# Segment attention with batch norm: four or six row tiles for each segment, chosen at run time

## The chip, the cores and the metric

The kernel runs on one core of a Trainium2 chip. A core has five engines that run their own instruction streams and wait for each other through semaphores: TensorE (matmuls, PE in the profile, its weight loads PEld), VectorE (DVE), ScalarE (ACT), GpSimd (POOL) and SyncE (SP, here only a queue for DMAs). The metric is device time in microseconds (us) of one execution. Three runs of the kernel before took 475.67, 477.01 and 477.55 us; the median, 477.01, is what the change is compared with.

## What is computed

There are 16384 tokens of 256 features, each with a segment id from 0 to 7. Ids are not sorted. A binary search over the ids gives each segment a start, and a token's slot is its index less that start; a token whose slot falls outside 0 to 3071 (negative ones wrap round) has none, and of several tokens on one slot one wins. Attention runs inside each segment over the slots that a token owns, with 32-wide queries and keys; then come a matmul with Wt, normalization over all tokens, relu, and the residual.

```python
q = feat @ Wq; k = feat @ Wk; v = feat @ Wv
starts = searchsorted(bids, arange(8))
pos = arange(N) - starts[bids]
qp, kp, vp = (zeros((8, 3072, c)).at[bids, pos].set(x) for x in (q, k, v))
scores = where(mask[:, None, :], einsum('bld,bmd->blm', qp, kp), -1e9)
rp = einsum('blm,bmd->bld', softmax(scores), vp)
t = rp[bids, pos] @ Wt
tn = (t - t.mean(0)) / sqrt(t.var(0) + 1e-5) * gamma + beta
out = feat + relu(tn)
```

On the reference's inputs the eight segments own 436, 511, 542, 726, 701, 698, 431 and 468 slots, 4513 in all. All other tokens read an empty slot, or one that another token owns.

## The kernel before

The function is segment_attention_bn_kernel. Rows of a segment are kept in FT = 6 row tiles of 128 (FW = 768 rows), whatever it owns; rows beyond the count are zero and are masked as keys. Four stages follow each other.

*Preparation* (lines 625 to 800, pool pp): loads of ids and weights, the binary search on VectorE, the counts n_bc of each segment and the running counts lcx. The longest segment becomes a register value (L794, L806), and L812 branches on it: the short path below, or a general path that these inputs don't take.

*Setting up the short path* (L813 to 846): the tiles xs (all tokens' rows, 48 row tiles), tk (results), acc (sums for the moments), xL, L, E and others are allocated and filled with zeros, xs by GpSimd (L831), the rest by VectorE (L832 to L837).

*Attention*, for segments 0 to 7 in one straight stream. load_list(e) (L859) builds a segment's list of tokens: masks ge and oh on VectorE (L866, L869), matmuls pc (L890), comparisons upto (L901), indices idx (L906), and then gathers by GpSimd of six row tiles of xs and of six columns reads_r (L911, L915, all through L850). project(b) (L917) transposes xs (px, L926), and makes queries and keys (pqk, L941), copied to q and k, and values (pv, L957; Wv and Wt have been multiplied together). attend(b) (L978) goes through two halves of 384 query rows: scores s (L994), four key tiles side by side on different rows of TensorE, then two; Exp by ScalarE into pr (L1000, two buffers); then for each of three query tiles six accumulating matmuls po (L1006), the reciprocal and the scaled row tk, and the two sums of acc (L1012 to L1023). After each half tk goes to DRAM (t_rows, L1038). reference_row (L964) subtracts a common row, from segment 0. The token tables (L1043 on) are worked out on VectorE after segment 0; load_others follows segment 1, and edge_selection (L1162) follows segment 2. The order within a block of straight code is made at build time by a scheduler, with program order as priority: ready work of later steps is drawn into gaps of earlier ones. Work inside a branch is not mixed with work outside it.

*The dense pass* (L1224 to 1359): every token's feature row is loaded, the relu of a common row is added and it is written back (f, L1299, L1320), while the rows of the lists are normalized (L1281 to L1287) and scattered into the output by GpSimd (L1336). A switch of many arms on GpSimd alone picks the order of the scatters.

The loop of attention, as it stands before the change:

```python
for b in range(NB):
    if b + 1 < NB:
        project(b + 1)
    if b + 2 < NB:
        load_list(b + 2, FT, xs[:, ts(b + 2, FT), :])
    attend(b)
```

Of the kernel before, what the change touches and what calls it, by code (L numbers as in the profile page):

```python
# [18 lines left out]
P = 128  # L19
# [12 lines left out]
QC = 384  # L32
QT = QC // P
# [497 lines left out]
def segment_attention_bn_kernel(  # L531
# [37 lines left out]
    LAST = TT * P - QC  # L569
# [5 lines left out]
    with ExitStack() as short:  # L575
# [13 lines left out]
        nc.vector.memset(eps_t, EPS)  # L589
        ones = keep.tile([P, P], F32, name="ones")  # L590
# [14 lines left out]
        arm_i = keep.tile([1, 1], I32, name="arm_i")  # L605
        ident = keep.tile([P, P], F32, name="ident")
        ecol = keep.tile([P, NB], F32, name="ecol")
        b_f = keep.tile([P, J], F32, name="b_f")

# [15 lines left out]
        with ExitStack() as prep:  # L625
# [46 lines left out]
            nc.vector.tensor_scalar(later_part[:, 1:2], part_i, 2 * NE, None, ALU.is_ge)  # L672

# [120 lines left out]
            nc.vector.tensor_copy(most_i, most)  # L794
            nc.vector.tensor_copy(cbeg, ps_c[:, 0, :])
# [16 lines left out]
        with tc.If(n_max < FW):  # L812
            with ExitStack() as path:  # L813
                fs = path.enter_context(tc.tile_pool(name="fs", bufs=1))
                xs = fs.tile([P, TT, D], F32, name="xs")
                tk = fs.tile([P, TT, D], F32, name="tk")
                idx = fs.tile([P, TT + LT], I32, name="idx")
                reads_r = fs.tile([P, TT], F32, name="reads_r")
                valid = fs.tile([P, TT + LT], F32, name="valid")
                mask = fs.tile([P, TT], F32, name="mask")  # L820
                rdens = fs.tile([P, TT], F32, name="rdens")
                acc = fs.tile([P, 2, D], F32, name="acc")
                sref = fs.tile([P, D], F32, name="sref")
                eidx = fs.tile([P, 1], I32, name="eidx")
                late = fs.tile([P, QT, P], F32, name="late")
                wE = fs.tile([NE, P], F32, name="wE")
                E = fs.tile([P, 2, D], F32, name="E")
                xL = fs.tile([P, LT, D], F32, name="xL")
                L = fs.tile([P, LT, D], F32, name="L")
                ridL = fs.tile([P, LT], I32, name="ridL")  # L830
                nc.gpsimd.memset(xs, 0.0)  # L831
                nc.vector.memset(acc, 0.0)  # L832
                nc.vector.memset(xL, 0.0)
                nc.vector.memset(ridL, NB * FW)
                nc.vector.memset(L, 0.0)
                nc.vector.memset(E, 0.0)
                nc.vector.memset(reads_r, 0.0)  # L837

# [8 lines left out]
                parts = {}  # L847
# [11 lines left out]
                def load_list(e, T, x):  # L859

# [3 lines left out]
                    ge = fw.tile([P, FW], F32, tag="ge", name=f"ge_{e}", bufs=1)  # L864
                    oh = fw.tile([P, FW], F32, tag="oh", name=f"oh_{e}", bufs=1)
                    nc.vector.tensor_scalar(  # L866
                        ge[:, 0 : T * P], ir, lcx[:, e, J : J + 1], None, ALU.is_ge
                    )
                    nc.vector.scalar_tensor_tensor(  # L869
                        oh[:, 0 : T * P], ir, cend[:, e : e + 1], ge[:, 0 : T * P],  # L870
# [6 lines left out]
                    if e < NB:  # L877
                        nc.vector.tensor_scalar(
                            mask[:, own_t], valid[:, own_t], 1.0, -NEG, ALU.subtract, ALU.mult
                        )  # L880
                    pad = fw.tile([P, FT], F32, tag="pad", name=f"pad_{e}")
                    nc.vector.tensor_scalar(
                        pad[:, 0:T], valid[:, own_t], 1.0, -float(N), ALU.subtract, ALU.mult
# [33 lines left out]
                def project(b):  # L917


                    x, v = xs[:, ts(b, FT), :], vs[b % 2]  # L920
                    xT = fw.tile([P, DH, FW], F32, tag="xT", name=f"xT_{b}", bufs=1)
                    for c in range(FT // 2):
                        for h in range(DH):
                            px = ps_a.tile([P, 2 * P], F32, tag="px", name=f"px_{b}")
                            for t in range(2):
                                nc.tensor.transpose(  # L926
                                    px[:, ts(t, P)], x[:, 2 * c + t, ts(h, P)], ident
                                )
                            if h == 0:
                                nc.scalar.copy(xT[:, h, ts(c, 2 * P)], px)  # L930
                            else:
                                nc.vector.tensor_copy(xT[:, h, ts(c, 2 * P)], px)


                    q = fw.tile([P, FW], F32, tag="q", name=f"q_{b}")
                    k = fw.tile([P, 2, P], F32, tag="k", name=f"k_{b}")
                    for c in range(FW // QC):
                        own_c = ts(c, QC)
                        pqk = ps_a.tile([P, QC], F32, tag="px", name=f"pqk_{b}")
                        for h in range(DH):  # L940
                            nc.tensor.matmul(  # L941
                                pqk, wqk[:, h, :], xT[:, h, own_c],
                                start=(h == 0), stop=(h == DH - 1),
                            )
                        nc.vector.tensor_copy(q[0 : 2 * DQ, own_c], pqk[0 : 2 * DQ, :])
                        nc.scalar.copy(q[2 * DQ : P, own_c], pqk[0 : 2 * DQ, :])
                        for u in range(QT):
                            t = c * QT + u
                            at, half = t % 4, P // 2 + DQ * (t % 2)
                            nc.vector.tensor_copy(  # L950
                                k[ts(at, DQ), t // 4, :], pqk[half : half + DQ, ts(u, P)]
                            )
                    for c in range(FT // 2):
                        pv = ps_a.tile([P, 2, D], F32, tag="px", name=f"pv_{b}")
                        for t in range(2):
                            for h in range(DH):
                                nc.tensor.matmul(  # L957
                                    pv[:, t, :], xT[:, h, ts(2 * c + t, P)], wvt[:, h, :],
                                    start=(h == 0), stop=(h == DH - 1),
                                )  # L960
                        nc.scalar.copy(v[:, 2 * c : 2 * c + 2, 0:D], pv)
                    parts[b] = (q, k)
# [15 lines left out]
                def attend(b):  # L978


                    q, k = parts[b]
                    v = vs[b % 2]
                    for c in range(FW // QC):
                        if b == NB - 1 and c == FW // QC - 1:
                            gather(E[:, 0, :], t_rows[0:LAST, :], eidx, LAST)
                            e_late = ps_a.tile([P, D], F32, tag="px", name="e_late")
                            root = fw.tile([P, 1], F32, tag="root", name="root")
                        pr = fw.tile([P, FT, QC], F32, tag="pr", name=f"pr_{b}")
                        for t0 in range(0, FT, 4):
                            quad = range(t0, min(t0 + 4, FT))  # L990
                            s = ps_s.tile([P, 4, PB], F32, tag="s", name=f"s_{b}")
                            for t in quad:
                                g = ts(t - t0, DQ)
                                nc.tensor.matmul(  # L994
                                    s[:, t - t0, 0:QC], k[g, t0 // 4, :], q[g, ts(c, QC)],
                                    start=True, stop=True,
                                )
                            for t in quad:
                                m = b * FT + t
                                nc.scalar.activation(  # L1000
                                    pr[:, t, :], s[:, t - t0, 0:QC], AF.Exp, bias=mask[:, m : m + 1]
                                )
                        for u in range(QT):
                            po = ps_o.tile([P, D + 1], F32, tag="po", name=f"po_{b}")
                            for t in range(FT):
                                nc.tensor.matmul(  # L1006
                                    po, pr[:, t, ts(u, P)], v[:, t, :],
                                    start=(t == 0), stop=(t == FT - 1),
                                )
                            at = b * FT + c * QT + u  # L1010
                            one = slice(at, at + 1)
                            nc.vector.reciprocal(rdens[:, one], po[:, D : D + 1])  # L1012
                            nc.vector.scalar_tensor_tensor(  # L1013
# [179 lines left out]
                for b in range(NB):  # L1193
                    if b + 1 < NB:
                        project(b + 1)
# [209 lines left out]
```

## Time and profile before

| What | Value |
|---|---|
| median of three runs | 477.01 us |
| span of the profiled execution | 474.8 us |
| PE busy | 361.2 us (76%) |
| DVE busy | 300.1 us (63%) |
| POOL busy | 174.6 us (37%) |
| ACT busy | 111.2 us (23%) |
| po matmuls (L1006), records | 576, 134.4 us |
| Exp (L1000) | 96, 577 ns each |
| gathers of xs and reads_r (L850) | 48 and 48, 1.05 us each |
| DMA moved | 53.14 MB |

The busy lines are shares of the whole span and average over stages with different limits, so the stages have to be read one by one. A line of the timeline gives the start, the duration, the engine, the source line, the operation with what it writes and reads, and in brackets how long its engine had been idle and whom it waited for. A float32 matmul shows as two records. A busy line of a stage gives each engine's busy time and, in parentheses, its instructions.

### The profile page before, as it was taken

The page shows a single profiled execution, that of the slowest core. Times are in us where ns is not written, and L with a number is a line of the kernel's source. Part 1 is how long each engine was busy: PE and PEld are TensorE (multiplying, and loading weights), DVE is VectorE, ACT ScalarE, POOL GpSimd, SP SyncE. Part 2 cuts the span into 40 slices and gives each one's busy share as a digit, 9 for nine tenths or more (in the row PEclk, how much of TensorE's full clock was granted, in tenths as well). Part 3 has the DMA queues.
Part 4 walks back from the last instruction along what each step waited for, and adds up shares of the span by engine and source line. Part 5 has one row for each costly group of instructions (what it writes and reads, how often), then busy time and mean ns, then how long its engine had stood idle before and what let it go on. Part 6 is the DMA issues. An engine that isn't in the chain of part 4 may idle for free. (4 is left out here: it accounts for less than half of the span.)

```text
span 474.8 us, 4852 instructions
## 1 busy us (share of the span) xinstructions
PE 361.2 (76%) x1465; PEld 237.1 (50%) x1465; DVE 300.1 (63%) x841; ACT 111.2 (23%) x232; POOL 174.6 (37%) x172
## 2 busy tenths in 40 slices
PE   4200368699999999999999999998891688989400
PEld 2000237467667667767677687676660243433200
DVE  6779868647879737446544644534447976977960
ACT  2000011223231432343243243324430011111000
POOL 1009360453804745407217127000002004667770
PEclk9999758979979999999999999999995566555555
DMA  5000100102312211203102101000119799999940
GB/s 92 1 6 0 34 10 1 44 4 65 101 50 68 68 48 51 77 0 94 35 0 72 34 27 49 33 2 33 55 56 381 318 351 421 378 416 412 413 170 8
DMA packets 21521, 53.14 MB, mean 112 GB/s; under 512 B 6670, under 2 KB 14176, under 8 KB 17386
## 3 DMA queue, kind: packets, MB, share of 16 engines
q1 hardware_dynamic: 10538, 24.98, 14.3%
q10 hardware_dynamic: 4224, 17.70, 9.8%
q0 software_dynamic: 6720, 10.03, 6.8%
q8 instruction: 14, 0.23, 0.2%
q14 instruction: 25, 0.20, 0.1%
HBM read 26.67 MB, written 29.92 MB: 119 GB/s over the span
## 5 line engine op out<-in xcount | busy, mean ns | idle before, releaser
L1006 PE MATMUL po<-vs,pr 128*128 128x257 f32 x576 | 134.4, 386 | 6.1 <-DVE acc L1023 5.0
L1006 PEld LDWEIGHTS po<-vs,pr 128*128 128x128 f32 x576 | 107.3, 191 | 32.7 <-ACT pr L1000 10.0
L850 POOL DMA_INDIRECT xs<-in_r_feat,idx x48 | 50.2, 1046 | 125.5 <-DVE upto L901 113.3
L1336 POOL DMA_INDIRECT out<-tk,idx x48 | 47.2, 984 | 52.6 <-DMA out<-f 34.2
L850 POOL DMA_INDIRECT reads_r<-reads_of,idx x48 | 51.0, 1062 | 14.6 <-issue 14.0
L1000 ACT ACTIVATE pr<-s,mask 128x384 f32<-128x384 f32 x96 | 48.7, 577 | 32.2 <-PE s L994 32.1
L1307 PE MATMUL pf<-y,hot 48*128 48x256 bf16 x128 | 35.2, 382 | 21.9 <-DVE f L1318 11.5
L1012 DVE RECIPROCAL rdens<-po 128x1 f32<-128x1 f32 x48 | 8.1, 168 | 64.2 <-PE po L1006 64.1
L957 PE MATMUL pv<-wvt,xT 128*128 128x256 f32 x192 | 46.5, 394 | 0.4
L994 PE MATMUL s<-q,k 32*128 32x384 f32 x192 | 44.3, 540 | 2.1 <-DVE k L950 2.1
L957 PEld LDWEIGHTS pv<-wvt,xT 128*128 128x128 f32 x192 | 36.7, 196 | 10.7 <-issue 5.9
L1318 DVE TENSOR_TENSOR f<-f,pf 128x512 f32<-128x512 f32 x48 | 30.9, 681 | 15.8 <-PE pf L1307 15.7
L1022 ACT ACTIVATE sq<-tk 128x256 f32<-128x256 f32 x48 | 20.0, 417 | 85.2 <-DVE tk L1013 72.5
L1307 PEld LDWEIGHTS <-hot 48*128 48x128 bf16 x128 | 13.7, 118 | 49.2 <-issue 45.8
L1312 PE MATMUL pf<-f,ident 128*128 128x256 f32 x64 | 36.0, 673 | 0.0
L926 PE MATMUL px<-ident,xs 128*128 128x128 f32 x96 | 19.7, 318 | 15.3 <-DMA xs<-in_r_feat,idx 7.5
L941 PE MATMUL pqk<-xT,wqk 128*128 128x384 f32 x64 | 28.0, 590 | 0.0
L890 PE MATMUL pc<-lcx,oh 128*128 128x130 f32 x102 | 16.3, 301 | 13.9 <-DVE oh L869 13.9
L926 PEld LDWEIGHTS px<-ident,xs 128*128 128x128 f32 x96 | 12.0, 154 | 28.4 <-issue 9.9
L1316 ACT COPY f<-pf 128x512 f32<-128x512 f32 x16 | 9.4, 585 | 71.2 <-PE pf L1312 71.2
L930 ACT COPY xT<-px 128x256 f32<-128x256 f32 x24 | 9.0, 373 | 69.2 <-PE px L926 69.2
L1013 DVE SCALAR_TENSOR_TENSOR tk<-po,rdens,sref 128x256 f32<-128x256 f32 x48 | 23.1, 481 | 1.5
(228 smaller groups left out, 406.9 us busy)
## 6 DMA issues: line engine op xcount, KB each, us to landing
f<-in_r_feat SPq DMA_DIRECT2D x16, 1024.0 KB, 9.8
out<-f ACTq DMA_DIRECT2D x16, 1024.0 KB, 9.1
t_rows<-tk SPq DMA_DIRECT2D x16, 384.0 KB, 2.6
eb<-edge_of SPq DMA_DIRECT2D x16, 96.0 KB, 2.9
xs<-in_r_feat,idx POOLq DMA_INDIRECT x48, 2.8
reads_r<-reads_of,idx POOLq DMA_INDIRECT x48, 2.4
out<-tk,idx POOLq DMA_INDIRECT x48, 8.4
wv_sb<-in_L_rec_Wv ACTq DMA_DIRECT2D x1, 256.0 KB, 3.2
```

The source lines that it names most:

```text
L850: nc.gpsimd.indirect_dma_start(out=dst, out_offset=None, in_=table, in_offset=bass.IndirectOffsetOnAxis(ap=ind, axis=0), bounds_check=n - ...
L926: nc.tensor.transpose(px[:, ts(t, P)], x[:, 2 * c + t, ts(h, P)], ident)
L941: nc.tensor.matmul(pqk, wqk[:, h, :], xT[:, h, own_c], start=(h == 0), stop=(h == DH - 1),)
L957: nc.tensor.matmul(pv[:, t, :], xT[:, h, ts(2 * c + t, P)], wvt[:, h, :], start=(h == 0), stop=(h == DH - 1),)
L994: nc.tensor.matmul(s[:, t - t0, 0:QC], k[g, t0 // 4, :], q[g, ts(c, QC)], start=True, stop=True,)
L1000: nc.scalar.activation(pr[:, t, :], s[:, t - t0, 0:QC], AF.Exp, bias=mask[:, m : m + 1])
L1006: nc.tensor.matmul(po, pr[:, t, ts(u, P)], v[:, t, :], start=(t == 0), stop=(t == FT - 1),)
L1013: nc.vector.scalar_tensor_tensor(tk[:, at, :], po[:, 0:D], rdens[:, one], sref, ALU.mult, ALU.subtract,)
L1307: nc.tensor.matmul(pf[:, u, :], hot[r, g % (NG // 2), i + u, :], y3[r, :], start=True, stop=not on_pe,)
L1312: nc.tensor.matmul(pf[:, u, :], ident, two[:, u, :], start=False, stop=True)
L1318: nc.vector.tensor_add(two, two, pf)
L1336: w = nc.gpsimd.indirect_dma_start(out=out, out_offset=bass.IndirectOffsetOnAxis(ap=idx[:, at : at + 1], axis=0), in_=y, in_offset=None, b ...
```

## The change

Every segment is given as many row tiles as it needs, out of two choices: four (TMIN) if it owns fewer than 512 slots, six otherwise. The choice is made at run time. For each half of the segments (PART = 4) a small number with one bit for each segment is counted (tiles_i), and attention becomes two switches of 16 arms, one for each combination; each arm holds the whole stream of four segments. It is for leaving out row tiles that hold nothing but zeros. Lists, gathers, and the projection of segments 0 and 4 keep six tiles in any case.

With it go these edits. Scores are taken 512 query rows wide (pr_a) and, for six tiles, 256 more (pr_b); both are single buffers. first_scores(b) takes the scores of the first four key tiles right after the projection, at the end of the segment before. Queries, keys and xT get fixed tiles; keys are copied ahead of queries. The zeros of xs, tk, acc, E, xL and L are written by ScalarE during preparation, before the branch, so the pool fs is opened earlier; tk needs zeros now in tiles that are not computed. The token tables split in two, the second part (edge_tables) after segment 1; load_others and edge_selection move to segments 2 and 4. The late matmuls of the last segment cover all its tiles instead of three, one behind each tile's sum. The rows of the other list are normalized in place (L instead of yL).

```diff
+            def zero(x):
+                nc.scalar.copy(x, nil.to_broadcast([P, x.shape[1]]))
+            for b in range(NB):
+                zero(xs[:, ts(b, FT), :].rearrange("p t d -> p (t d)"))
+            for b in range(NB):
+                zero(tk[:, b * FT + TMIN : (b + 1) * FT, :].rearrange("p t d -> p (t d)"))
+            for x in (acc, E, xL, L):
+                zero(x.rearrange("p t d -> p (t d)"))
...
+            nc.vector.scalar_tensor_tensor(
+                tiles, n_bc[0:1, 0:NB], float(TMIN * P), powers, ALU.is_ge, ALU.mult
+            )
+            nc.vector.tensor_reduce(
+                part, tiles.rearrange("x (a b) -> x a b", b=PART), AX.X, ALU.add
+            )
+            nc.vector.tensor_copy(tiles_i, part)
...
-                nc.gpsimd.memset(xs, 0.0)
-                nc.vector.memset(acc, 0.0)
-                nc.vector.memset(xL, 0.0)
-                nc.vector.memset(ridL, NB * FW)
-                nc.vector.memset(L, 0.0)
-                nc.vector.memset(E, 0.0)
-                nc.vector.memset(reads_r, 0.0)
...
+                pr_a = fw.tile([P, FT, QA], F32, name="pr_a", bufs=1)
+                pr_b = fw.tile([P, FT, FW - QA], F32, name="pr_b", bufs=1)
+                tiles = [
+                    nc.values_load(
+                        tiles_i[0:1, a : a + 1],
...
+                def scores(b, items):
+                    q, k = qs[b % 2], ks[b % 2]
+                    s = ps_s.tile([P, 4, PB], F32, tag="s", name=f"s_{b}")
+                    for i, (t, c, w) in enumerate(items):
+                        g = ts(t % 4, DQ)
+                        nc.tensor.matmul(
+                            s[:, i, 0:w], k[g, t // 4, :], q[g, c : c + w], start=True, stop=True
+                        )
...
+                def attend(b, T):
+                    w = (T - TMIN) * P
...
+                    if T > TMIN:
+                        scores(b, [(4, 0, QA), (5, 0, QA), (2, QA, w), (3, QA, w)])
+                        scores(b, [(0, QA, w), (1, QA, w), (4, QA, w), (5, QA, w)])
+                    for u in range(T):
+                        sums(b, u, T, e_late)
...
+                def project(b, T):
+                    turn(b, T)
+                    queries_keys(b, 0, QA)
+                    if T > TMIN:
+                        queries_keys(b, QA, (T - TMIN) * P)
+                    values(b, T)
...
                 load_list(0, FT, xs[:, ts(0, FT), :])
-                project(0)
+                project(0, FT)
+                first_scores(0)
                 reference_row()
                 load_list(1, FT, xs[:, ts(1, FT), :])
...
+                for a in range(NB // PART):
...
+                    for arm in tc.Switch(tiles[a], 1 << PART):
+
+                        T = [FT if arm >> i & 1 else TMIN for i in range(PART)] + [FT]
+                        for i in range(PART):
+                            b = a * PART + i
+                            if b + 1 < NB:
+                                project(b + 1, T[i + 1])
+                            if b + 2 < NB:
+                                load_list(b + 2, FT, xs[:, ts(b + 2, FT), :])
+                            attend(b, T[i])
+                            if b + 1 < NB:
+                                first_scores(b + 1)
+                            if b == 0:
+                                token_tables()
+                            if b == 1:
+                                edge_tables()
+                            if b == 2:
+                                load_others()
+                            if b == 4:
+                                edge_selection()
...
-                yL = fin.tile([P, LT, D], F32, name="yL")
...
-                    normal(yL[:, two, :], xL[:, two, :], L[:, two, :], min(2, LT - at))
+                    normal(L[:, two, :], xL[:, two, :], L[:, two, :], min(2, LT - at))
```

## The prediction

> **What bounds the kernel now.** I read the 40 slices first, then busy time by stage, then the order of instructions inside stages.
>
> ```profile
> PE   4200368699999999999999999998891688989400
> PEld 2000237467667667767677687676660243433200
> DVE  6779868647879737446544644534447976977960
> ```
>
> TensorE is full from slice 12 to 27, VectorE is fuller before that, and both are uneven in the last quarter. Columns below: stretch, its length, then busy us (instructions) of PE, PEld, DVE, ACT, POOL, then clock, DMA share, GB/s.
>
> ```profile
> 34.50:86.40 51.90, 25.13 (x88) 17.19 (x88) 42.28 (x111) 4.45 (x10) 23.02 (x15) 0.80 0.04 10
> 86.40:125.00 38.60, 34.13 (x148) 24.80 (x149) 22.59 (x88) 10.73 (x23) 21.45 (x21) 0.91 0.19 50
> 125.00:165.50 40.50, 39.14 (x165) 26.79 (x163) 33.52 (x89) 13.23 (x29) 19.37 (x17) 0.92 0.22 68
> 165.50:232.20 66.70, 65.94 (x304) 47.97 (x304) 33.96 (x110) 23.89 (x52) 30.44 (x30) 1.00 0.17 49
> 232.20:330.90 98.70, 96.91 (x441) 69.61 (x439) 45.95 (x141) 35.96 (x77) 23.93 (x24) 1.00 0.11 34
> 330.90:353.40 22.50, 20.70 (x101) 15.31 (x100) 10.31 (x27) 8.37 (x18) 1.00 (x1) 1.00 0.13 41
> 353.40:474.80 121.40, 70.75 (x201) 30.70 (x200) 85.61 (x154) 11.77 (x20) 53.43 (x54) 0.55 0.82 323
> ```
>
> These are: start up to the first sum of attention; segment 0; segment 1; 2 and 3; 4 to 6; 7; the dense pass. From 165.5 to 330.9 TensorE works 98% of the time: its work is the price. The dense pass moves data (DMA share 0.82). The order of the start:
>
> ```profile
> 34.34 0.14 DVE L794 CAST most_i<-most 1x1 int32<-1x1 f32 x1
> 35.54 10.34 POOL L831 MEMSET xs<- 128x12288 f32 x1 [32.91 <-issue]
> ...
> 38.17 8.12 DVE L866 TENSOR_SCALAR ge<-iota_r,lcx 128x768 f32<-128x768 f32 x1
> ...
> 47.41 0.61 DVE L866 TENSOR_SCALAR ge<-iota_r,lcx 128x768 f32<-128x768 f32 x1
> ...
> 53.86 1.20 POOL L850 DMA_INDIRECT xs<-in_r_feat,idx  x1 [7.51 <-DVE upto L901]
> ```
>
> The same operation lasts 8.12 us while GpSimd fills, 0.61 later. From 34.34 to the first gather at 53.86 nothing else can start. TensorE in a steady segment (33.4 us long):
>
> ```profile
> 213.34 8.10 PE L1006 MATMUL po<-vs,pr 128*128 128x257 f32 x36
> 221.37 0.93 PE L994 MATMUL s<-q,k 32*128 32x384 f32 x8
> ...
> 234.95 2.85 PE L941 MATMUL pqk<-xT,wqk 128*128 128x384 f32 x8
> ...
> 238.67 5.71 PE L957 MATMUL pv<-wvt,xT 128*128 128x256 f32 x24
> 244.22 1.78 PE L890 MATMUL pc<-lcx,oh 128*128 128x130 f32 x12
> ```
>
> Each float32 matmul is two records. By tile, 212.5 to 245.9 has po 16.45, s 5.48, pv 5.66, pqk 2.85, px 1.91, pc 1.74 us.
>
> **What the skill says.** "SBUF — State Buffer", section "SBUF: two separate sides": GpSimd and a VectorE operation in a two-port mode share a port pair under an exclusive lock, so the later one waits out the whole instruction. The trace agrees: 8.12 us against 0.61. "TensorE: Matmul & The Clock Gate", Part 3: matmuls on different 32-row groups run side by side. Agreed: four of s as one group take 0.93 us, two take 0.91. "Runtime: NRT & Kernel Launch", "Instruction fetch mechanics": a taken branch outside the fetched window waits until a DMA has brought the target. This trace shows no such branch by itself.
>
> **The change, part by part.** *How many tiles.* On the reference's inputs the segments own 436, 511, 542, 726, 701, 698, 431, 468 slots. Four (0, 1, 6, 7) are under 512 and take four tiles; 0 is still projected with six.
>
> *Sums of a short segment.* 16 products instead of 36: 16.45 x 16/36 = 7.3 us. pv: 5.66 x 4/6 = 3.8; pqk the same way 1.9; px 1.3; pc stays 1.74. Scores: one group of four, 512 wide: 0.92 x 512/384 = 1.2 us if side by side. Together 17.2, plus 1 us of gaps as now: 18.2 instead of 33.4. *A long segment*: three score groups, 1.2 + 1.2 + 0.6; together 31.7 and 1 of gaps: 32.7, nearly as now.
>
> *Start.* The GpSimd fill and six VectorE fills leave this place; ScalarE writes nearly all zeros before the branch, VectorE the two small ones. The price, from "ScalarE: Activation LUTs", section "What ACT_TABLE_LOAD costs" (186 ns and 0.833 ns an element): eight of 1536 elements 1.47 us, ten of 512 0.61, two of 768 0.83: 19.5 us, an estimate. ScalarE is busy 2.8 of the first 34.5 us, so it is hidden. ge then ends at about 37.3 instead of 46.2: 8.9 saved. The token tables (L1049 and on), now inside the arms, no longer cut in before upto (1.2) and between pqk and k (2.5), and Exp of segment 0, whose scores now go ahead of the reference row, no longer starts 1.7 before the first sum. Against it 0.5 for the counting operations (three of some 0.14 and a load). Net 13.8 saved, before the switch.
>
> *Two switches.* Each engine jumps by itself. From below, the branch at L812 took 1.07 us with its load (34.48 to 35.55 on VectorE); from above, add a fetch like a DMA's landing (eb 2.9 us) and a cold TensorE clock for some us: 6. I take 3.5 for the first, where segment 1's gather is waited for anyway, and 5 for the second. All later work of each engine queues behind its jump. First sum at 86.4 - 13.8 + 3.5 = 76.1.
>
> *What the arms keep in.* The token tables can't fill VectorE's idle time before the switch any more: 12 passes of about 1.2 us, a reduction of 1.87 and small ones, 17.5. For segment 0 VectorE has these, a list 4 (ge 0.61, oh 1.01, six upto of 0.35, small ones), a projection 2.7 (two xT of 0.42, q 0.7, four k of 0.29) and four row tiles of sums at 1.7 (rdens 0.17, three operations of 0.48, gaps): 31. For segment 1: a list 4, a six-tile projection 4.1, sums 6.9 and the edge tables 6: 21. That is 52 against 39 of TensorE (17.5 and 21.6), so VectorE bounds this stage: with 6 of waits 58 us (79.1 now), to 134. Segments 2 and 3: 66, to 200. Switch: 205.
>
> *Part two.* Segment 4: projection 10.4, scores 3, sums 16.45, list 1.74 and a gap: 32.6. Segment 5 with the short projection of 6: 10.4 - 3.5 = 6.9, in all 29.1. Segment 6 without list and with 7's projection: 16.4. Segment 7: sums 7.3, four late matmuls 2.2, and 3 for Exp, which writes the single pr_a only after segment 6's sums: 12.5. Sum 90.6 (121.2 now), to 296. The edge selection (eight of 0.91 + 1.12, 16 us of VectorE) lies in segment 4: VectorE 35 against 32.6, which segment 5 (18 against 29) takes up. Moved pools, six late tables, and L in place of yL: nothing, beside TensorE or the dense pass.
>
> *Dense pass.* Unchanged: 121.4, and 1 for the join. 418 us of span. The timed median lies 2.2 above the profile's span: **420**.
>
> **Rivals.** (1) *Cheap jumps, VectorE hidden*: jumps of 2 us, segments 0 and 1 in 50: 407. For it: DVE is idle within every steady segment (17.39 of 33.4 busy). Against: the tables come all at once. 17%. (2) *Jumps that cost all through*: every block of 256 instructions is waited for (the Runtime page's block size): part one has some 900 on TensorE, both parts seven blocks, 2.9 each: 20 more, 440. For it: arms are large and padded. Against: straight code within an arm is fetched ahead. 19%. (3) *Slower than before*: pr_a is not doubled, so each segment's Exp (six of 0.7, with latencies 6 us) lies bare: 48 for eight, with (2) 420 + 68 = 488. Against: the next projection (7 to 10 us of TensorE) lies between. 4%. The forecast keeps 60%.
>
> **How the numbers follow.** The likeliest is 420. The low end, 404, takes in (1) with shorter waits; the high end, 442, the switches' upper price twice (7 more), VectorE's waits doubled (6) and much of (2). Outside remain (3) and tails of (1) and (2). Faster 0.95, same 0.01, slower 0.04.
>
> **What would show it.** ge near 0.6 us at about 36.5; 416 records of sums instead of 576 (4 x 16 + 4 x 36, twice); first sum near 76; segments 0 and 1 with DVE above 85%; short segments in part two 16 to 18 us; a hole of 3 to 6 us on all engines near 200; the dense pass 121. It is wrong if the holes at the switches pass 10 us, if idle before po falls to pr (Exp) at every segment, or if the dense pass starts later than the sums' end allows.

## The result and the profile after

The changed kernel takes **437.26 us** (median of four runs, 434.82 to 438.22), the kernel before, measured beside it, 476.34: a ratio of 0.919, 95% interval 0.913 to 0.925. The forecast was 420, so the direction was right and 17 us of the expected 57 did not come. The profiled execution is the fastest of the four: 434.82 us, span 432.9. Some executions come out slower than the others of the same kernel, and the ratios, here and below, leave those out, so that a ratio can differ a little from that of the medians.

The slices of the page first, as for before:

```profile
PE   1143684996697999999599989999706888989200
DVE  6796124996962267556457954646479866596950
PEclk9996597998697799999579999999855675555555
```

A slice is now 10.8 us. TensorE is no longer full from one end of attention to the other: it dips to 5 in the twentieth slice (206 to 216 us). The granted clock is 0.6, 0.7 and 0.7 in three of the slices between 108 and 151 us, and 0.5 and 0.7 in the two from 206 on. The first of these slices lies in segments 0 and 1, the others are the places that the forecast lacks.

The stages, cut at the end of each segment's last sum (columns as in the prediction; the start up to the first sum, segments 0 and 1, 2, 3, the second switch with 4, 5, 6 and 7, dense pass):

```profile
33.80:75.70 41.90, 24.21 (x92) 15.92 (x93) 15.51 (x67) 6.30 (x13) 16.68 (x19) 0.74 0.09 23
75.70:127.20 51.50, 42.85 (x171) 29.98 (x169) 43.31 (x143) 11.07 (x24) 26.73 (x22) 0.88 0.11 34
127.20:169.70 42.50, 38.68 (x158) 26.52 (x158) 19.73 (x74) 12.64 (x27) 20.55 (x22) 0.88 0.21 63
169.70:203.60 33.90, 33.89 (x163) 24.88 (x162) 19.11 (x65) 12.26 (x26) 17.95 (x18) 1.00 0.18 53
203.60:249.50 45.90, 39.56 (x157) 26.24 (x157) 32.39 (x77) 14.57 (x28) 13.36 (x12) 0.85 0.21 64
249.50:280.00 30.50, 29.33 (x138) 21.16 (x138) 15.79 (x52) 10.98 (x24) 15.57 (x16) 1.00 0.14 43
280.00:307.30 27.30, 25.41 (x117) 18.11 (x116) 16.95 (x43) 10.77 (x22) 1.46 (x2) 1.00 0.13 44
307.30:432.90 125.60, 71.13 (x199) 30.30 (x198) 85.30 (x152) 11.17 (x18) 53.23 (x54) 0.54 0.81 315
```

Segments 2, 3 and 4 do nearly the same work on TensorE, six tiles each. Segment 3 takes 33.9 us with TensorE always busy at clock 1.00. Segment 2 takes 42.5 and segment 4 45.9, both at a lower clock, with idle time, and with more busy time for the same matmuls. The forecast against this table:

| Stage | Forecast, us | Measured, us | Difference |
|---|---|---|---|
| start to the first sum | 76.1 | 75.75 | -0.3 |
| segments 0 and 1 | 58 | 51.5 | -6.5 |
| segments 2 and 3 | 66 | 42.5 + 33.9 | +10.4 |
| second switch and segment 4 | 5 + 32.6 | 45.9 | +8.3 |
| segment 5 | 29.1 | 30.5 | +1.4 |
| segments 6 and 7 | 28.9 | 27.3 | -1.6 |
| dense pass and join | 122.4 | 125.6 | +3.2 |
| span | 418 | 432.9 | +14.9 |

The remaining 2.4 us lie between this execution (434.82, 1.9 above its span, where the forecast had 2.2) and the median of the runs.

The start of the changed kernel, in order of time, answers to the lines of before:

```profile
33.56 0.13 DVE L834 CAST most_i<-most 1x1 int32<-1x1 f32 x1
33.62 0.15 DVE L845 CAST tiles_i<-part 1x2 int32<-1x2 f32 x1
34.63 0.69 DVE L906 TENSOR_SCALAR oh<-iota_r,lcx 128x768 f32<-128x768 f32 x1 [0.87 <-DVE tiles_i L845]
...
40.20 1.20 POOL L892 DMA_INDIRECT xs<-in_r_feat,idx  x1 [5.29 <-DVE idx L952]
```

The comparison that took 8.12 us takes 0.69, and the first gather leaves at 40.20 instead of 53.86. The sums are 320 records on pr_a and 96 on pr_b, 416 as forecast.

TensorE around segment 2 (start, duration, what; in brackets its idle time and whom it waited for):

```profile
112.53 2.07 PE L1018 MATMUL s<-q,k 32*128 32x512 f32 x2 [4.84 <-DVE q L995]
...
135.97 0.90 PE L974 MATMUL px<-ident,xs 128*128 128x128 f32 x3 [2.69 <-DMA xs<-in_r_feat,idx]
...
141.00 5.37 PE L985 MATMUL pqk<-xT,wqk 128*128 128x512 f32 x8
```

and the same pqk one segment later:

```profile
177.91 2.75 PE L985 MATMUL pqk<-xT,wqk 128*128 128x512 f32 x8
```

A wait for the gathered rows of segment 3, then the same eight records at half speed. The gathers themselves, from GpSimd's timeline:

```profile
124.94 0.99 POOL L892 DMA_INDIRECT xs<-in_r_feat,idx  x1 [16.25 <-DVE upto L947]
126.24 1.18 POOL L892 DMA_INDIRECT xs<-in_r_feat,idx  x1 [0.30 <-issue]
127.73 1.19 POOL L892 DMA_INDIRECT xs<-in_r_feat,idx  x1 [0.30 <-issue]
129.22 1.00 POOL L892 DMA_INDIRECT reads_r<-reads_of,idx  x1 [0.30 <-issue]
...
133.12 1.00 POOL L892 DMA_INDIRECT xs<-in_r_feat,idx  x1 [0.30 <-issue]
```

GpSimd had been idle for 16 us until the list was ready (upto), so the gathers begin only as segment 2 begins; and three gathers of reads_r, which nobody waits for yet, stand ahead of the last three of xs.

At the second switch, ScalarE:

```profile
204.74 2.42 ACT L1023 ACTIVATE pr_a<-s,mask 128x512 f32<-128x512 f32 x4
211.41 1.28 ACT L1096 ACT_TABLE_LOAD   x1 [4.26 <-issue]
212.71 0.20 ACT L1096 ACTIVATE root<-eps_t 128x1 f32<-128x1 f32 x1
212.81 0.35 ACT L978 COPY xT<-px 128x256 f32<-128x256 f32 x1
...
217.39 1.28 ACT L1023 ACT_TABLE_LOAD   x1
...
316.08 1.28 ACT L1330 ACT_TABLE_LOAD   x1 [9.01 <-DVE mom L1328]
```

and TensorE there:

```profile
213.22 1.12 PE L974 MATMUL px<-ident,xs 128*128 128x128 f32 x4 [3.11 <-ACT xT L978]
...
218.52 4.09 PE L985 MATMUL pqk<-xT,wqk 128*128 128x512 f32 x8
```

"issue" means that the engine waited for nothing that the profile shows in the idle 4.26 us: this is the jump. VectorE shows 4.06 at the same place; TensorE stands for 2.61 us from 204.67 on. Behind the jump comes something that the forecast did not speak of. Before, the early square root that brings in its function table (L1036) read a column of sq, and so could only run at the end. Now it reads the constant eps_t (L1096) and depends on nothing, so the scheduler put it at the top of the arm: the table is loaded, the copy of xT waits behind it (TensorE waits 3.11 us for that copy), Exp has to load its table again, and at 316.08 the dense pass loads the square root's once more.

### The profile page after: what moved, and what is told of

It is laid out like the page before. It is cut to its first block, busy times and chain, and to the rows that moved or that the text cites. A ratio compares the mean times of both kernels' runs of the same rounds, so it can differ in the third digit from the quotient of the medians.

```text
span 432.9 us, 4300 instructions
## 1 busy us (share of the span) xinstructions
PE 313.1 (72%) x1195; PEld 197.4 (46%) x1195; DVE 274.3 (63%) x801; ACT 110.1 (25%) x205; POOL 167.8 (39%) x179
## 5 line engine op out<-in xcount | busy, mean ns | idle before, releaser
L1051 PE MATMUL po<-vs,pr_a 128*128 128x257 f32 x320 | 78.3, 391 | 2.9 <-ACT pr_a L1023 2.3
L1051 PEld LDWEIGHTS po<-vs,pr_a 128*128 128x128 f32 x320 | 59.3, 193 | 17.3 <-issue 4.4
L1018 PE MATMUL s<-q,k 32*128 32x512 f32 (+1 forms) x128 | 36.8, 593 | 6.0 <-DVE q L995 6.0
L1004 PE MATMUL pv<-wvt,xT 128*128 128x256 f32 x168 | 40.8, 398 | 0.0
L974 PEld LDWEIGHTS px<-ident,xs 128*128 128x128 f32 x84 | 11.7, 170 | 42.6 <-issue 19.6
L1023 ACT ACTIVATE pr_a<-s,mask 128x512 f32<-128x512 f32 x40 | 24.7, 687 | 17.8 <-PE s L1018 17.7
L978 DVE COPY xT<-px 128x256 f32<-128x256 f32 x21 | 8.9, 422 | 29.5 <-PE px L974 29.5
L985 PE MATMUL pqk<-xT,wqk 128*128 128x512 f32 (+1 forms) x52 | 25.4, 634 | 0.1
L1051 PE MATMUL po<-vs,pr_b 128*128 128x257 f32 x96 | 21.8, 381 | 0.3 <-DVE tk L1056 0.3
L992 DVE COPY k<-pqk 32x128 f32<-32x128 f32 x42 | 12.2, 291 | 14.0 <-PE pqk L985 13.1
L1390 PEld LDWEIGHTS pf<-f,ident 128*128 128x128 f32 x64 | 15.4, 292 | 12.2 <-issue 7.6
```

Source lines behind the costliest of these rows:

```text
L974: nc.tensor.transpose(px[:, ts(t, P)], xs[:, b * FT + t0 + t, ts(h, P)], ident)
L985: nc.tensor.matmul(pqk[:, 0:w], wqk[:, h, :], xT[:, h, own_c], start=(h == 0), stop=(h == DH - 1),)
L1004: nc.tensor.matmul(pv[:, t, :], xT[:, h, ts(t0 + t, P)], wvt[:, h, :], start=(h == 0), stop=(h == DH - 1),)
L1018: nc.tensor.matmul(s[:, i, 0:w], k[g, t // 4, :], q[g, c : c + w], start=True, stop=True)
L1023: nc.scalar.activation((pr_b if c else pr_a)[:, t, 0:w], s[:, i, 0:w], AF.Exp, bias=mask[:, m : m + 1],)
L1051: nc.tensor.matmul(po, pr[:, t, ts(r, P)], v[:, t, :], start=(t == 0), stop=(t == T - 1))
```

## The experiments

Each kernel is the changed one with the edit shown, but for the fourth. The first four ran on one chip, beside a kernel before of 474.63 us. The next four and the last four ran on two others, where the kernel before took 514.99 and 512.66 us; these two are alike, so ratios to the kernel before are set side by side, and stages of attention only where they differ by more than these groups do among themselves.

**Arms fixed when the kernel is built** (12 and 3, the arms that these inputs take): no switch is left, and work can be ordered across the borders.

```diff
-                    for arm in tc.Switch(tiles[a], 1 << PART):
+                    for arm in tc.Switch((12, 3)[a], 1 << PART):
```

> The two choices of an arm are made at build time (the arms that the inputs take, 12 and 3), so nothing is dispatched and the whole of attention is one block again. Theory A (jumps and block ends cost): the trace after has holes of 4.06 to 4.42 us on VectorE, ScalarE and TensorE at each jump, a cold clock behind the second, and the token tables can't be drawn forward; without them 437 falls to 420 to 427. Rival B (the single-buffered scores and VectorE's queue are the loss, the jumps are hidden beside waits for gathers): 433 to 437.

Measured: 422.88 us, ratio 0.882 (0.875 to 0.889); span 422.1. Theory A: by the medians 14.4 us, by the spans of the profiled executions 10.8, are the price of the two switches, with all that the scheduler orders otherwise when they are gone. The first sum comes at 72.4 instead of 75.75; segments 3 and 4 together take 72.6 us instead of 79.8. Part of the latter is not the jump: the square root on eps_t is drawn forward here too, but to 34.6 us, so that no table load stands in segment 4. Segment 2 is not better for it (44.0).

**The square root tied to data again**:

```diff
-                        nc.scalar.activation(root, eps_t, AF.Sqrt)
+                        nc.scalar.activation(root, E[:, 1, 0:1], AF.Sqrt)
```

> Only the input of the square root that loads ScalarE's table is changed, from a constant to the last result E, as the kernel before had it tied to the last sum. Theory A: the square root now runs first in the second arm, between the jump and the first xT copy, so one table load (1.28 us) stands there on the path of TensorE, and a third one stands ahead of root_v in the dense pass (1.28 us): 2.5 to 4 us less, 433 to 435. Rival B: both lie beside other waits (the pqk at a cold clock, the loads of f): 437, within 1.

Measured: 432.94 us, ratio 0.909 (0.903 to 0.915), 4.3 less than the changed kernel: theory A, a shade more than it named. ScalarE at the end of attention in this kernel:

```profile
306.24 0.42 ACT L1064 ACTIVATE sq<-tk 128x256 f32<-128x256 f32 x1 [1.93 <-DVE tk L1056]
306.68 1.28 ACT L1096 ACT_TABLE_LOAD   x1
308.00 0.20 ACT L1096 ACTIVATE root<-E 128x1 f32<-128x1 f32 x1
315.49 0.51 ACT L1330 ACTIVATE root_v<-mom,eps_t 128x256 f32<-128x256 f32 x1 [7.28 <-DVE mom L1328]
```

The table is there 7 us before root_v needs it. Two loads remain of four. By the profiled spans (430.2 against 432.9) the stage of the second switch is 1.5 shorter and the time from the last sum to the end 2.3; the stages between differ by about 1 to and fro.

**Six tiles in every arm**: the switches and all edits stay, but nothing is left out.

```diff
-                        T = [FT if arm >> i & 1 else TMIN for i in range(PART)] + [FT]
+                        T = [FT] * (PART + 1)
```

> All arms take six tiles for every segment; switches, zeros by ScalarE and the order stay. Theory A (the gain is the left out tiles): four segments get back some 15 us each, less what VectorE hides in segments 0 and 1: 437 + 40 to 55 = 477 to 492, so about the kernel before or slower. Rival B (most of the gain is the start): 437 + 15 = 452 or less.

Measured: 478.52 us, ratio 1.008 (1.006 to 1.011). All the gain of the change is the tiles that it leaves out (theory A); what the other edits save and what they cost all but cancels, with 3.9 us left as a cost. The stages of this kernel (segments 0 and 1, 2, 3, second switch and 4):

```profile
89.30:148.80 59.50, 58.22 (x267) 43.81 (x265) 42.86 (x145) 18.52 (x40) 23.72 (x23) 1.00 0.15 46
148.80:182.90 34.10, 33.72 (x159) 24.61 (x158) 18.96 (x71) 12.30 (x26) 11.69 (x13) 1.00 0.14 45
182.90:216.70 33.80, 33.79 (x162) 24.85 (x162) 19.11 (x65) 12.19 (x26) 17.91 (x18) 1.00 0.18 53
216.70:261.70 45.00, 39.66 (x157) 26.45 (x157) 32.39 (x77) 14.55 (x28) 13.65 (x11) 0.85 0.21 65
```

Segment 2, with the same work as in the changed kernel, takes 34.1 us here, and stage 4 again 45. Its list of segment 3 is gathered from 134.94 on, 14 us before segment 2 begins, in the same order of three and three; in the changed kernel they begin at 124.94, 2 us before. So the 8.4 us that segment 2 loses in the changed kernel are not work of segment 2: they come from work for later segments, the list and its gathers above all, that two long segments used to cover and two short ones do not.

**The zeros alone**: the kernel before, with its fills of xs, acc, E, xL and L moved to ScalarE ahead of the branch.

```diff
+            for b in range(NB):
+                zero(xs[:, ts(b, FT), :].rearrange("p t d -> p (t d)"))
+            for x in (acc, E, xL, L):
+                zero(x.rearrange("p t d -> p (t d)"))
...
-                nc.gpsimd.memset(xs, 0.0)
-                nc.vector.memset(acc, 0.0)
```

> The kernel before with only the zeros moved: xs, acc, E, xL and L filled by ScalarE ahead of the branch, the two small ones by VectorE there. Theory A: the first gather moves from 53.9 to 42 to 44 us (the 8.12 us operation falls to 0.61, and 2.6 us of fills go), and all behind it moves too: 476 - 10 = 464 to 468. Rival B (VectorE's token tables and the next list then hold up segment 0 and 1 instead): 472 to 476.

Measured: 467.29 us, ratio 0.980 (0.975 to 0.985), first sum at 78.82 instead of 86.40. Theory A, though the first gather leaves at 45.06, not at 42 to 44, since the preparation itself ends 2.1 us later here. These 7.3 us need no switch at all.

**Only the second part straight**:

```diff
-                    for arm in tc.Switch(tiles[a], 1 << PART):
+                    for arm in tc.Switch((tiles[0], 3)[a], 1 << PART):
```

> Only the second switch is taken away (its arm fixed at build time); the first stays. It splits what both together cost, 14.4 us (437.3 less 422.9). Theory A: the first jump hides beside segment 1's gather, so most lies at the second: 437 falls to 425 to 428. Rival B (both jumps cost alike, and the first one also keeps the token tables out of early gaps): 430 to 432.

Measured: 478.9 us, ratio 0.931 (0.925 to 0.938): both theories missed, and it is slower than the changed kernel (0.897 in the last group). VectorE's and then TensorE's timeline of this kernel:

```profile
219.31 1.12 DVE L1228 TENSOR_SCALAR hot<-eb,emod 128x1024 bf16<-128x1024 bf16 x1 [3.57 <-DMA eb<-edge_of]
...
236.90 1.12 DVE L1228 TENSOR_SCALAR hot<-eb,emod 128x1024 bf16<-128x1024 bf16 x1 [0.89 <-DMA eb<-edge_of]
...
239.54 0.42 DVE L978 COPY xT<-px 128x256 f32<-128x256 f32 x1
```

```profile
240.02 0.69 PE L974 MATMUL px<-ident,xs 128*128 128x128 f32 x2 [22.17 <-DVE xT L978]
```

The scheduler queued the whole edge selection ahead of a copy of xT, and TensorE stood for 22 us. The run tells nothing of the jump. It tells that what a switch costs is confounded with how the scheduler orders the work around it.

**A hint for the first switch**, which fetches the arm's code ahead:

```diff
+                hints = [
+                    tc.switch_hint(
+                        {e: tiles[0] for e in (ENG.PE, ENG.DVE, ENG.Activation, ENG.Pool, ENG.SP)},
+                        1 << PART, "part0",
+                    ),
+                    None,
+                ]
...
-                    for arm in tc.Switch(tiles[a], 1 << PART):
+                    for arm in tc.Switch(tiles[a], 1 << PART, hint=hints[a]):
```

> The first switch gets a hint for prefetch of its arm right after its register has been loaded, some 35 us ahead; nothing else changes. Theory A (the hole of 4.39 us on VectorE and of 4.42 on TensorE is a fetch of the arm's code): VectorE's hole falls to 1 to 1.5 us; TensorE's stays near 4, since it also waits for the gather of segment 1; 435 to 437 in all. Rival B (the hole is the dispatch and the load of registers): the hole stays above 4 us and the time 437.

Measured: ratio 0.890 (0.880 to 0.900), no difference from the changed kernel's 0.897. VectorE's first instruction in the arm, first in the changed kernel, then here (where lines stand nine further down):

```profile
75.15 0.62 DVE L906 TENSOR_SCALAR oh<-iota_r,lcx 128x768 f32<-128x768 f32 x1 [4.39 <-issue]
```

```profile
73.83 0.62 DVE L915 TENSOR_SCALAR oh<-iota_r,lcx 128x768 f32<-128x768 f32 x1 [0.76 <-issue]
...
75.49 0.45 PE L983 MATMUL px<-ident,xs 128*128 128x128 f32 x1 [4.36 <-DMA xs<-in_r_feat,idx]
```

VectorE's hole of 4.39 us is the fetch of code: with the hint 0.76 are left, and of the ten packets that the instruction queues start between 62 and 82 us in the changed kernel six are left. But TensorE waits 4.36 for segment 1's gathered rows with or without it (4.42), and the first sum is not earlier (77.25). The first jump lies wholly beside that gather.

**Token tables ahead of the first switch**:

```diff
+                token_tables()
                 for a in range(NB // PART):
...
-                            if b == 0:
-                                token_tables()
```

> The token tables (17.5 us of VectorE) stand ahead of the first switch, where VectorE has idle time, instead of inside the arms. Theory A (in the arms they hold up k and q of segment 2, where TensorE waits 4.84 us for VectorE, and the list of segment 3): 3 to 8 us less, 429 to 434. Rival B (they are then late to the jump, and the gathers of GpSimd are what segment 2 waits for): 436 to 441.

Measured: ratio 0.893 (0.886 to 0.900), no difference. Segments 0 and 1 are 47.7 us, but the first sum comes at 79.64, so segment 1 ends at 127.4, in the changed kernel at 127.2. Segment 2 takes 43.1: the tables are not what makes it long, as rival B had it.

**Gathers of reads written behind attend**:

```diff
+                list_reads(0)
...
+                                list_reads(b + 1)
```

> The six gathers of reads_r of a list are put behind the six of xs, instead of among them (they are 1.3 us apart, so the last rows of xs are issued up to 4 us earlier). Theory A (behind a short segment the gathers are the longest chain: TensorE waits 18.7 us for xs in the trace after, 7.5 before): 3 to 7 us less, 430 to 434. Rival B (VectorE's queue sets when a list is ready, the gathers only follow): 436 to 438.

Measured: ratio 0.883 (0.873 to 0.893), not clear. In the arm that runs, the scheduler still put three gathers of reads between those of xs, so this tested nothing; segment 2 takes 42.6 us.

**The changed kernel once more**, as the measure of the last group:

> The changed kernel again, as the measure for the three kernels beside it. Both theories: a ratio of 0.912 to 0.925 to the kernel before if the chip is like the first; 0.88 to 0.90 if it is like the one of the second group, where the kernel before took 515 us. First sum near 75.8 us, second segment's end 124 to 127, third segment 42 to 43 us long, in any case.

Measured: 460.68 us, ratio 0.897 (0.891 to 0.902). The first sum comes at 76.59, segment 1 ends at 126.06, and segment 2 (the "third" of these texts) takes 41.0, 1 us less than expected.

**All gathers of xs ahead of those of reads**, forced by data:

```diff
+                        idx_c = fw.tile([P, FT], I32, tag="idx_c", name=f"idx_c_{e}")
+                        nc.vector.tensor_scalar(idx_c, idx[:, at : at + T], 0, None, ALU.add)
...
-                            gather(reads_r[:, m : m + 1], reads_of, idx[:, m : m + 1], N)
+                            gather(reads_r[:, m : m + 1], reads_of, idx_c[:, t : t + 1], N)
```

> The gathers of reads take their rows from a copy of the list that needs both halves of it, so all six gathers of xs go out ahead of the six of reads (before: three, three, three, three, at 1.3 us each). Theory A (the wait of TensorE for xs at 133 us and the cold clock after it make the third segment long): the last three gathers of xs go out 3.9 us earlier, the wait of 2.7 us ends, pqk of the third segment falls from 5.37 towards 2.75 and s by 0.95; the third segment takes 36 to 39 us instead of 42.6 and the kernel 4 to 7 us less than the changed kernel. Theory B (VectorE's tables and the late list hold the segment up, the gathers only follow): third segment within 1.5 us of 42.6, the kernel within 2 us of the changed one.

Measured: 453.14 us, ratio 0.883 (0.879 to 0.888); 7.5 us under the changed kernel beside it. TensorE's lines of segment 2 in this kernel:

```profile
130.71 0.55 PE L976 MATMUL px<-ident,xs 128*128 128x128 f32 x3 [0.61 <-DMA xs<-in_r_feat,idx]
...
133.70 4.25 PE L987 MATMUL pqk<-xT,wqk 128*128 128x512 f32 x8
```

The wait of 2.7 us is 0.6, and TensorE's idle time in segment 2 is 1.9 to 2.2 us in the three kernels with this edit (this one and the two that follow), and segment 2 takes 37.8, 38.0 and 39.3 us in them. In the seven with short segments, a switch and the old order it takes 40.9 to 43.1, with 3.0 to 4.0 idle. So theory A holds, for some 3.5 us on the average, but not in all its links: pqk does not fall. It is 4.25 here and 4.21 in the changed kernel beside it (2.71 us of wait), and 4.2 to 5.4 in the seven. What falls is the idle time and the matmuls right behind it (s 1.12 instead of 2.02). Nor is the wait all of it: with the tables ahead of the switch it was 0.83 us, and segment 2 still took 43.1, at a mean clock of 0.84. The other 4 of the 7.5 are not in segment 2, and where they come from stays open; the kernel with the gathers of reads written behind attend had the old order and the same ratio, 0.883, so no more than segment 2's own time is put down to the gathers.

**The same with the square root tied and hints for both switches**, and (the "next run" of its text) **without the hints**:

> The kernel of the next run and a hint for each of the two switches, placed ahead of attention. Theory A (the first hole lies beside the gather of xs and costs nothing, the second is on the path): VectorE's hole at the first switch falls from 4.4 to under 1 us and the first sum stays within 1.5 us of 76; the second hole falls too, TensorE's wait there by 2 to 4 us, the kernel 2 to 5 us under the next run. Theory B (the second hint comes 170 us ahead of its jump and has been overwritten by then): hole at the second switch still about 4 us, the kernel within 2 us of the next run. Rival C: the hints' own fetches disturb, the kernel is slower than the next run.

> The kernel with all gathers of xs ahead of those of reads, and the square root of the dense pass tied to a row of E so that it can't be moved into the second arm. Theory A: the gains add, 8 to 11 us under the changed kernel (4.3 from the square root as measured, 4 to 7 from the gathers). Theory B: only the square root's, 3.5 to 5.5 us under it. Two activation table loads instead of four in any case.

Measured: 449.86 us, ratio 0.875 (0.868 to 0.882) without hints, and 450.51 us, 0.875 (0.870 to 0.880) with them. Both edits together are worth 10.8 us (theory A of the second text), 2.4% of the changed kernel beside them, and this is the fastest version that still chooses at run time. The hints are worth nothing (theory B of the first text): with two of them VectorE's hole at the first switch is 3.32 us (3.54 without), and at the second 3.93 (4.05). That the second hint displaces the first one's code is a reading of these numbers, not shown.

## Why the forecast was right, and where it was short

The tiles left out are the gain, as the forecast had it, and 437.26 lies in its range of 404 to 442, near the upper end. Two stages came out 10.4 and 8.3 us too long. That segments 0 and 1 came out 6.5 too short has nothing to do with these two and made up for part of them: this is luck. The range's upper end also holds a wrong sum: both switches at their upper price of 6 are 3.5 more than the 8.5 taken, not 7.

**Zeros and the comparison: right.** 8.9 us were forecast, the first sum moved by 7.6 in the run with the zeros alone, and the comparison took 0.69 us. ScalarE wrote the zeros between 6.46 and 24.18 us, 17.7 for the 19.5 estimated, beside other work as forecast.

**The first switch: right in sum, other in kind.** 3.5 us were taken for the jump. The jump's hole is 4.4 us, and it costs nothing, since the gathers of segment 1 end later. But without a switch the first sum comes 3.3 us earlier, because work of both sides can mix: there the sums of segment 0 start at 72.42, ahead of segment 1's transposes at 77.95, and in the changed kernel they start behind the first of these. The price is that of a wall, not of a fetch.

**VectorE in segments 0 and 1: right in kind, its size too large.** 52 us of VectorE work were added up; the window shows 43.3 in 51.5, 84%. The forecast's "DVE above 85%" is just missed. Of TensorE's 8.65 idle us in this stage 5.6 are waits for VectorE and 2.5 for gathered rows; that VectorE bounds it is in part still an argument, since moving 17.5 us of tables out of it gained nothing.

**Segments 2 and 3: the step that failed.** "Segments 2 and 3: 66" took both as steady segments bound by TensorE. That holds for segment 3 (33.9), though its scores were put at 3.0 us, as three groups of four side by side, and took 5.9: the scheduler set transposes between them, and two records alone take as long as eight together.

```profile
169.66 1.14 PE L1018 MATMUL s<-q,k 32*128 32x512 f32 x8
...
173.74 1.12 PE L1018 MATMUL s<-q,k 32*128 32x512 f32 x2
```

Segment 2 took 42.5: with segment 1 ending at 127.2 us instead of 148.8 (six tiles everywhere), the chain of list, upto and six gathers, which has its own length, ended inside segment 2. The run with six tiles everywhere shows that the 8.4 us belong to the shortening; the run with the gathers reordered wins back 3.5 of them. On TensorE this shows as idle time of 3.8 us and then a cold clock: pqk 5.37 against 2.75, s 7.31 against 5.94, px 3.17 against 2.13. "TensorE: Matmul & The Clock Gate", section "HAM oscillation — how this bites in real kernels", describes this: waits for DMA, of more than some 3.4 us, that throttle the clock to one half. The half agrees (5.37 against 2.75), the length does not: here 2.69 us, with 1.13 us some 6 us earlier, were followed by 10 us at a granted clock of 0.50 (135.9 to 146.1 us). Why pqk stayed partly cold after the shorter waits is open.

**The second switch: the other failed step.** 5 us were taken, from a range whose upper end was 6; with segment 4 the stage came out 8.3 longer than forecast. The hole itself, 4.1 to 4.3 us on VectorE and ScalarE, is inside the range. Missing was what follows it: the hoisted square root with its two table loads (1.5 us by the run without it), and TensorE's cold clock after the hole (pqk 4.09 against 2.75, s 9.45 against 5.94). Taken net, with segment 3, which the straight kernel fills with later work, the second switch costs 7.2 us of the profiled span, the table loads included.

**Segments 5 to 7: right.** 57.8 us against 58.0. The Exp of segment 7 is bare for only 0.83 us, not 3; in the whole kernel TensorE's sums waited 2.3 us for Exp, against the 48 of the rival of bare Exps (488), which is thereby refuted.

**Dense pass: 3.2 us long.** The forecast counted "L in place of yL" and the rest as nothing, and didn't see that L1096 had lost the tie that kept it in its place. The load at 316.08 is 1.28 us on the chain from mom to root_v. "ScalarE: Activation LUTs", section "What ACT_TABLE_LOAD costs", gives 1283 ns, and the trace agrees. Tying it again takes 2.3 us off the end; what the rest of the 3.2 is stays open.

**The rival of dear jumps** named 440 and came nearest in number, but by another way. It had every block of code waited for. Code traffic did grow; the instruction queues of the page, before, after and with the arms fixed:

```profile
q8 instruction: 14, 0.23, 0.2%
q14 instruction: 25, 0.20, 0.1%
```

```profile
q14 instruction: 51, 0.42, 0.3%
q8 instruction: 16, 0.26, 0.3%
```

```profile
q8 instruction: 11, 0.18, 0.2%
q14 instruction: 26, 0.20, 0.2%
```

67 packets instead of 39, and 37 without switches; 10 of the 67 start between 62 and 82 us and 18 between 198 and 213, around the two jumps. But TensorE was idle for 0.0 us in segment 3 and 1.2 in segment 5, so on the first chip code inside an arm was not waited for. That the number comes so near the measured one is chance.

## What to carry to other kernels

When a stage is shortened, look at what it used to cover: a chain of list, index and gather keeps its length, and can come out in the next stage. A warming instruction needs a data tie that keeps it in its place, or a scheduler moves it to where its table load is dear. A run-time branch is priced as a wall in the order of work and a cold TensorE after it; here its fetch cost nothing at the first switch, where a transfer lay beside it.

## What the hardware showed that was not expected

The jump into an arm left VectorE idle for 4.06 to 4.39 us and ScalarE for 4.26, and one hint cut VectorE's to 0.76, with no gain in time, while two hints did not (3.32 and 3.93).

The groups ran on three chips, each at another time, and their times differ. The kernel before took about 475 us on one, 515 and 513 on two others; the changed kernel 437 and, on one of these two, 461. Whether the chip or the time makes the difference no run tells. From the last sum to the end, the changed kernel took 127.1 us on the first, the fastest version 135.1 on another. On the two others VectorE also had idle stretches of 2.9 to 6.1 us ahead of rdens inside an arm, at about the same places of the program in every kernel, that the changed kernel on the first chip doesn't show. One from the kernel with the gathers reordered, TensorE and then VectorE:

```profile
282.25 2.77 PE L1053 MATMUL po<-vs,pr_b 128*128 128x257 f32 x12
288.47 1.76 PE L1053 MATMUL po<-vs,pr_b 128*128 128x257 f32 x7 [3.45 <-remote]
```

```profile
287.64 0.17 DVE L1057 RECIPROCAL rdens<-po 128x1 f32<-128x1 f32 x1 [4.69 <-remote]
```

By their records the sums were complete at 285.0, and VectorE had been idle since 282.95. But the profile models the ends of matmuls. The trace also keeps the times of semaphore updates, and TensorE's has one at 287.62, 0.02 us before VectorE goes on; all but one of the other such stretches end the same way. So it is TensorE whose sums came late: on the first chip, in the same sums, these updates come 0.43 us apart, here, between 283.3 and 287.6 us, first 0.7 and then 2.1, at a granted clock recorded as 1.00. It is not a fetch of code on the two instruction queues, which start no packet between 274.9 and 289.4. What slowed TensorE stays open.
